# The last stage of an adaLN block with routed experts: two sums per batch added by transfers, by TensorE or by VectorE

## The chip, the core and the metric

The kernel runs on one core of a Trainium2 chip. The metric is the device time of one launch in microseconds (us). The kernel before took 437.91 us as the median of 3 runs (436.64 to 440.29). The profile comes from one further execution.

## The reference, cut to what matters

The block takes 8 batches of 256 tokens with 256 features, all in fp32. Attention adds to `x`; then comes a feed-forward part with 16 routed experts (each token goes to 4 of them) and one shared expert of width 352. Two of its lines are the subject of this document:

```
y = jnp.einsum('teh,ehd,te->td', h, w2, cw)          # the routed experts, weighted
z = jax.nn.silu(xf @ sw1) * (xf @ sw3) @ sw2         # the shared expert
...
x = x + gb * (y + z)                                 # gb: one row of 256 per batch
```

So each output needs the sum of a token's four expert results, the shared expert's result, one multiplication by the gate `gb`, and one addition of the residual `x`.

## The kernel before

**The work up to the last stage.** Attention and routing run first, on all engines, in an order that is written out by hand. Then tiles of 128 tokens of one expert each go through five steps: `fetch` (a load of sorted rows by the queue of SyncE, SP), `turn`, `up`, `flip` and `down` (TensorE with ScalarE and VectorE). `down` ends with a tile of 128 rows, and `add_some` (L1207) adds these to their tokens' rows in DRAM by an indirect transfer with addition, issued by GpSimd (POOL). To keep neighbouring additions apart there are two tables in DRAM, `sums[0]` and `sums[1]`, and the tiles go to them in turn. Each of the two holds a part of `y`, and both have to be added at the end. There are 70 such additions in the profiled execution. Transfers that POOL issues go through the queue q0 of the profile, those of SP through q1.

**The shared expert.** For batches 0 to 5 it is computed earlier and added to the residual `xs[b]` with its gate. For batches 6 and 7 (`NEXT` = 6) it is left to the end. `hidden(b0, 2, i)` (L1215) takes chunk `i` of three of the hidden width (128, 128 and 96 columns) for two batches at once: four matmuls with 512 columns (L1224), a Silu on ScalarE (L1230) and a product on VectorE (L1231) that makes the tile `hs`. `shared(b)` (L1235) takes the three `hs` tiles to one batch's result in PSUM, in six matmuls with 256 columns (L1240).

**The last stage (L1312 to L1337).** SP loads, for batch 0 to 7 in order, a quarter of a megabyte from `sums[0]` and another from `sums[1]` into the halves of a tile `got` (L1319), 16 loads in all. The loads wait for the last additions to DRAM. Meanwhile TensorE computes `hidden` and `shared` for batches 6 and 7. Then VectorE makes for each batch a pass `got[0] + got[1]` (L1330), for batches 6 and 7 another that adds the shared expert from PSUM (L1332), a pass that multiplies by the gate (L1333), and a pass that adds `xs[b]` (L1336). SP stores the result (L1337).

**What sets the order.** Up to the end of the first expert tiles the three compute engines follow the order of the code. In the last stage a scheduler of the compiler orders each engine's instructions by its own estimates, so VectorE mixes passes of several batches with those of `hidden`. Each engine then works through its queue in that order: an instruction that waits holds up all behind it. SP issues its 16 loads first and its 8 stores after them.

Of the kernel before, what the change touches and what calls it, by code (L numbers as in the profile page):

```python
# [9 lines left out]
F32 = mybir.dt.float32  # L10
# [4 lines left out]
ALU = mybir.AluOpType  # L15
# [3 lines left out]
P = 128  # L19
B, S, HID = 8, 256, 256  # L20
NT = S // P
# [31 lines left out]
SHC = [(c, min(P, SH - c)) for c in range(0, SH, P)]  # L53
# [8 lines left out]
NEXT = 6  # L62
# [12 lines left out]
BEHIND = mybir.DependencyInfo(mybir.DependencyClass.NoSync, mybir.DependencyReason.DATA)  # L75
# [3 lines left out]
def kernel(  # L79
# [18 lines left out]
    nc = tc.nc  # L98
# [18 lines left out]
    xs = []  # L117
# [3 lines left out]
    def load_x(b):  # L121
# [16 lines left out]
        out=bias_sb,  # L138
        in_=expert_bias.rearrange("(o e) -> o e", o=1).to_broadcast([P, E]),
# [7 lines left out]
    ident = const.tile([P, P], F32)  # L147
# [9 lines left out]
    for lo, n in ((0, P), (P, Q0)):  # L157
        nc.gpsimd.affine_select(
            out=maskb[:, lo : lo + n], in_=maskb[:, lo : lo + n], compare_op=ALU.is_ge, fill=HIDDEN,
# [3 lines left out]
            out=maskb[:, lo : lo + n], in_=maskb[:, lo : lo + n], compare_op=ALU.is_ge, fill=HIDDEN,  # L163
# [9 lines left out]
    for pr in probs:  # L173
# [7 lines left out]
        out=lowG, in_=lowG, compare_op=ALU.is_gt, fill=0.0,  # L181
# [6 lines left out]
        out=before, in_=before, compare_op=ALU.is_gt, fill=0.0,  # L188
# [11 lines left out]
    for m in range(SUMS):  # L200
# [4 lines left out]
            out=spread[:, m, :].rearrange("p (j d) -> p j d", d=D),  # L205
            in_=spread[:, m, :].rearrange("p (j d) -> p j d", d=D),
# [11 lines left out]
    def apart(ins, group):  # L218
# [12 lines left out]
    first = const.tile([P, E], F32)  # L231
    nc.gpsimd.iota(
        first, pattern=[[CAP, E]], base=1, channel_multiplier=0,
# [13 lines left out]
    start = const.tile([E, 1], F32)  # L247
    nc.gpsimd.iota(
        start, pattern=[[0, 1]], base=-E * CAP, channel_multiplier=CAP,
# [5 lines left out]
        out=upto, in_=upto, compare_op=ALU.is_ge, fill=0.0,  # L255
# [9 lines left out]
    sums = [tc.dram_tile([NTOK + P, HID], F32, name=f"sums_{i}") for i in range(2)]  # L265
# [76 lines left out]
    with ExitStack() as actx:  # L342
# [701 lines left out]
        for b in range(B):  # L1044
# [63 lines left out]
        ps_y = ctx.enter_context(tc.tile_pool(name="ps_y", bufs=2, space=PSUM))  # L1108
        small_ps[0] = ps_r
        gbs = gp.tile([P, B, HID], F32)  # L1110
        nc.sync.dma_start(
            out=gbs, in_=gates_d[1:2].rearrange("a b d -> a (b d)").to_broadcast([P, B * HID])
        )

        xts, hts, sels, zs = {}, {}, {}, {}
# [99 lines left out]
        def hidden(b0, nb, i):  # L1215

            c, n = SHC[i]
            pool, tag = ((ps_t, "t"), (ps_u, "u"), (ps_t, "t"))[i]
            pus = [
                pool.tile([P, 2, S], F32, tag=tag, name=f"us_{b0}_{i}_{a}")[:, 0:nb] for a in range(2)  # L1220
            ]
            for a in range(2):
                for k in range(NK):
                    nc.tensor.matmul(  # L1224
                        out=pus[a][:n], lhsT=sw13_sb[:, k, a, c : c + n],
                        rhs=h2T[:, k, b0 : b0 + nb, :],
                        start=(k == 0), stop=(k == NK - 1),
                    )
            h = fp.tile([P, 2, S], F32, tag="hs", name=f"hs_{b0}_{i}")[:, 0:nb]
            nc.scalar.activation(h[:n], pus[0][:n], AF.Silu)  # L1230
            nc.vector.tensor_tensor(h[:n], h[:n], pus[1][:n], ALU.mult)  # L1231
            for b in range(b0, b0 + nb):
                hids[b, i] = h[:, b - b0]

        def shared(b):  # L1235

            pz = ps_y.tile([P, NT, HID], F32, tag="y", name=f"pz_{b}")
            for t in range(NT):
                for i, (c, n) in enumerate(SHC):
                    nc.tensor.matmul(  # L1240
                        out=pz[:, t, :], lhsT=hids[b, i][:n, t * P : (t + 1) * P],
                        rhs=sw2_sb[:n, i, :],
                        start=(i == 0), stop=(i == len(SHC) - 1),
                    )
            return pz

# [8 lines left out]
        def shared_next(b):  # L1255

            pz = shared(b)
            nc.vector.tensor_tensor(
                pz, pz, gbs[:, b, :].unsqueeze(1).to_broadcast([P, NT, HID]), ALU.mult
            )  # L1260
            nc.vector.tensor_tensor(xs[b], xs[b], pz, ALU.add)
# [8 lines left out]
        def shared_some(b0):  # L1270

            for i in range(len(SHC)):
                hidden(b0, 2, i)
                yield
            for b in range(b0, b0 + 2):
                shared_next(b)
                yield
# [34 lines left out]
    tctx.close()  # L1312
    ep = ctx.enter_context(tc.tile_pool(name="ep", bufs=B))
    fp = ctx.enter_context(tc.tile_pool(name="fp_end", bufs=len(SHC)))
    gots = []
    for b in range(B):
        got = ep.tile([P, 2, NT, HID], F32, tag="got", name=f"got_{b}")
        for i in range(2):
            nc.sync.dma_start(  # L1319
                out=got[:, i], in_=sums[i][b * S : (b + 1) * S, :].rearrange("(p t) d -> p t d", p=P)  # L1320
            )
        gots.append(got)
    for b0 in range(NEXT, B, 2):
        for i in range(len(SHC)):
            hidden(b0, 2, i)
        for b in range(b0, b0 + 2):
            zs[b] = shared(b)
    for b, got in enumerate(gots):
        o = got[:, 0]
        nc.vector.tensor_tensor(o, got[:, 0], got[:, 1], ALU.add)  # L1330
        if b in zs:
            nc.vector.tensor_tensor(o, o, zs[b], ALU.add)  # L1332
        nc.vector.tensor_tensor(  # L1333
            o, o, gbs[:, b, :].unsqueeze(1).to_broadcast([P, NT, HID]), ALU.mult
        )
        nc.vector.tensor_tensor(o, o, xs[b], ALU.add)  # L1336
        nc.sync.dma_start(out=out[b].rearrange("(t p) d -> p t d", p=P), in_=o)  # L1337


# [54 lines left out]
```

## Time and profile before

| | |
|---|---|
| median of 3 runs (lowest, highest) | 437.91 us (436.64, 440.29) |
| the profiled execution's own time | 436.18 us |
| its span | 434.2 us |
| granted TensorE clock, mean over the span | 0.973 |
| busy share: PE, VectorE (DVE), GpSimd (POOL), ScalarE (ACT) | 91%, 59%, 55%, 44% |
| last POOL instruction ends | 404.05 us |
| first load of the last stage issued | 408.67 us |
| last VectorE pass ends | 430.88 us |

Times in views of the trace count from the start of the span, so the last stage is what lies between about 400 and 434 us. "PEclk" or "granted clock" is the share of full speed at which TensorE was let run. "PEld" is the load of weights into TensorE. A matmul in fp32 shows as two instructions, so 6 matmuls of `shared` are 12 rows. "Idle before" is what an engine waited before an instruction, and the arrow names what ended the wait. The share of DMA is the mean busy share of the core's 16 transfer engines; it can pass 1 a little where packets overlap.

### The profile page before, as it was taken

How to read it: one execution, taken by the hardware profiler on the slowest of the kernel's cores; microseconds unless marked ns; L12 is line 12 of the kernel's file. 1: busy time of each engine (PE TensorE's matmuls, PEld its weight loads, DVE VectorE, ACT ScalarE, POOL GpSimd, SP SyncE). 2: the span in 40 equal slices, each digit the busy share in tenths (PEclk: the TensorE clock that was granted, in tenths of full speed). 3: DMA queues.
4: the chain of work that ended last, by engine and by line, in shares of the span. 5: the costliest groups of instructions: out<-in, count | busy, mean ns of one | idle time of the engine just before them, and what ended most of it. 6: DMA issues, size and time to landing. Idle time of an engine off the chain costs nothing.

```text
span 434.2 us, 8867 instructions
## 1 busy us (share of the span) xinstructions
PE 396.6 (91%) x2790; PEld 282.3 (65%) x2790; DVE 256.5 (59%) x937; ACT 192.6 (44%) x445; POOL 239.3 (55%) x232
## 2 busy tenths in 40 slices
PE   3779999899999989799999999999999999997963
PEld 3445777677788855567776575667777777775332
DVE  4586887989887745456763343354445444443096
ACT  1446687777767743245432212134334344433100
POOL 8255444648878755056754346766666666656100
PEclk9998999999999999999999999999999999999778
DMA  8999996012131321535554226667766666675493
GB/s 257 368 362 306 323 231 171 2 54 61 63 103 61 110 95 61 175 109 130 141 129 110 54 53 103 77 109 122 115 107 116 117 104 120 113 116 79 95 381 128
DMA packets 53214, 60.05 MB, mean 138 GB/s; under 512 B 5304, under 2 KB 48176, under 8 KB 53040
## 3 DMA queue, kind: packets, MB, share of 16 engines
q1 hardware_dynamic: 40016, 40.86, 32.2%
q0 software_dynamic: 13152, 18.62, 23.5%
q8 instruction: 24, 0.39, 0.4%
q14 instruction: 22, 0.18, 0.1%
HBM read 31.77 MB, written 27.69 MB: 137 GB/s over the span
## 4 chain that ended last, share of the span: by engine, by line
PE 43%; DMA 8%; DVE 4%; issue 2%; ACT 1%; SPq 0%; DVEq 0%
PE u L1167 17%; PE py L1193 13%; DMA sums<-yr,to 5%; PE us L1224 4%; PE ph L1182 3%; PE xt L1135 3%; PE pz L1240 2%; DMA xr<-rows_d 2%; DMA got<-sums 1%; DVE got L1330 1%; DVE got L1333 1%; DVE got L1336 1%; DVE got L1332 0%; ACT L1174 0%; ACT L895 0%
## 5 line engine op out<-in xcount | busy, mean ns | idle before, releaser
L1207 POOL DMA_INDIRECT sums<-yr,to x70 | 109.6, 1565 | 54.3 <-DVE yr L1200 11.9
L1167 PE MATMUL u<-w,xT 128*128 x288 | 98.9, 467 | 2.2 <-ACT xT L1137 2.2
L976 POOL DMA_INDIRECT rows_d<-pay,idx x64 | 63.9, 998 | 64.6 <-PE ph L1182 24.2
L1193 PE MATMUL py<-w_sb,hT 88*128 x280 | 72.1, 380 | 0.0
L1167 PEld LDWEIGHTS u<-w,xT 128*128 128x128 f32 x288 | 49.9, 193 | 19.2 <-ACT xT L1137 2.4
L1137 ACT COPY xT<-xt 128x256 f32<-128x256 f32 x73 | 26.9, 372 | 60.7 <-PE xt L1135 60.7
L1175 DVE TENSOR_TENSOR h<-h,u 128x176 f32<-128x176 f32 x72 | 24.2, 337 | 47.3 <-ACT h L1174 47.1
L1193 PEld LDWEIGHTS py<-w_sb,hT 88*128 88x128 f32 x280 | 47.7, 190 | 3.8
L1174 ACT ACTIVATE h<-u 128x176 f32<-128x176 f32 x72 | 22.8, 317 | 57.9 <-PE u L1167 57.2
L1200 DVE TENSOR_SCALAR yr<-py,w 128x256 f32<-128x256 f32 x70 | 33.6, 479 | 11.1 <-PE py L1193 10.8
L1224 PE MATMUL us<-h2T,sw_sb 128*128 128x512 f32 (+1 forms) x72 | 35.6, 640 | 3.5 <-PEq L1306 2.7
L399 POOL TENSOR_TENSOR rstd<-rstd,nhalf 128x24 f32<-128x24 f32 x8 | 33.8, 4220 | 0.7
L1141 DVE SCALAR_TENSOR_TENSOR both<-eno,whose,xr 128x16 f32<-128x16 f32 x73 | 16.9, 232 | 27.2 <-DMA xr<-rows_d 26.9
L1182 PEld LDWEIGHTS ph<-ident,h 128*88 128x88 f32 x142 | 17.1, 122 | 21.4 <-issue 12.2
L516 PE MATMUL pq<-wqkv_sb,hT 128*128 128x384 f32 x64 | 27.7, 565 | 2.9 <-ACT hT L375 2.0
L1135 PE MATMUL xt<-ident,xr 128*128 128x128 f32 x146 | 28.2, 276 | 0.0
L1182 PE MATMUL ph<-ident,h 128*88 128x128 f32 x142 | 27.2, 274 | 0.6 <-DVE h L1175 0.6
L1224 PEld LDWEIGHTS us<-h2T,sw_sb 128*128 128x128 f32 (+1 forms) x72 | 13.8, 196 | 21.2 <-issue 19.2
L1184 ACT COPY hT<-ph 88x256 f32<-88x256 f32 x71 | 26.1, 367 | 2.5 <-PE ph L1182 2.2
L1135 PEld LDWEIGHTS xt<-ident,xr 128*128 128x128 f32 x146 | 20.4, 144 | 8.8 <-issue 2.9
L634 ACT ACTIVATE probs<-probs 128x640 f32<-128x640 f32 x32 | 23.6, 737 | 1.0
L631 ACT ACTIVATE probs<-sc 128x640 f32<-128x640 f32 x32 | 22.2, 694 | 4.1 <-PE sc L622 4.1
(231 smaller groups left out, 658.3 us busy)
## 6 DMA issues: line engine op xcount, KB each, us to landing
xr<-rows_d SPq DMA_DIRECT2D x75, 144.0 KB
w<-in_w_dram SPq DMA_DIRECT2D x16, 352.0 KB
sums<-none SPq DMA_DIRECT2D x2, 2176.0 KB
got<-sums SPq DMA_DIRECT2D x16, 256.0 KB
w_sb<-in_w_dram SPq DMA_DIRECT2D x8, 352.0 KB
rows_d<-none SPq DMA_DIRECT2D x1, 2304.0 KB
x<-in_x_dram SPq DMA_DIRECT2D x8, 256.0 KB
out_dram<-got SPq DMA_DIRECT2D x8, 256.0 KB
```

The lines of the kernel that those rows point to most:

```text
L399: in_turn("own", nc.gpsimd.tensor_tensor(out, out, nhalf[:, 0 : in_.shape[-1]], ALU.pow))
L516: ins = nc.tensor.matmul(out=pq[:, 0 : NH * D], lhsT=hT[:, k, t * P : (t + 1) * P], rhs=wqkv_sb[:, k, :], start=(k == 0), stop=(k == NK - 1),)
L976: ins = nc.gpsimd.indirect_dma_start(out=rows_d[:, :], out_offset=bass.IndirectOffsetOnAxis(ap=idx[:, t, k : k + 1], axis=0), in_=pay[:, t ...
L1135: nc.tensor.transpose(pt[:, k, :], x[:, k * P : (k + 1) * P], ident)
L1137: nc.scalar.copy(xT, pt)
L1167: ins = nc.tensor.matmul(out=pu, lhsT=xT[:, k, :], rhs=w13[:, k, bass.ds(e, 1), :].rearrange("p o h -> p (o h)"), start=(k == 0), stop=(k ...
L1182: nc.tensor.transpose(ph[:, i, :], h[:, i * HALF : (i + 1) * HALF], ident)
L1184: nc.scalar.copy(hT, ph)
L1193: nc.tensor.matmul(out=py, lhsT=h[:, i, :], rhs=w2_sb[:, i, bass.ds(e, 1), :].rearrange("p o d -> p (o d)"), start=(i == 0), stop=(i == 1),)
L1200: nc.vector.tensor_scalar(y, py, w, None, ALU.mult)
L1207: ins = nc.gpsimd.indirect_dma_start(out=sums[len(added) % 2][:, :], out_offset=bass.IndirectOffsetOnAxis(ap=to[:, 0:1], axis=0), in_=y, i ...
L1224: nc.tensor.matmul(out=pus[a][:n], lhsT=sw13_sb[:, k, a, c : c + n], rhs=h2T[:, k, b0 : b0 + nb, :], start=(k == 0), stop=(k == NK - 1),)
```

## The change

Only the last stage changes, and the functions `hidden` and `shared` for it.

- **Batches 2, 3, 4, 5.** SP loads only the first sum. The second one is added to it in SBUF by a transfer with addition that GpSimd issues (it waits until SP's load has landed). VectorE's pass L1330 is gone for these four.
- **Batches 6, 7.** Both sums are loaded as before. TensorE adds them into the PSUM tile of the shared expert: two matmuls of the identity with 512 columns each open the accumulation, and `shared` goes on in it. VectorE's passes L1330 and L1332 are gone for these two; the gate's multiplication reads PSUM.
- **Batches 0, 1.** As before, with three passes on VectorE.
- **Orders.** SP's loads come in the order 2, 3, 0, 4, 5, 1, 6, 7. VectorE's order is written out: products of `hidden` for chunks 0 and 1, batch 0, batch 1, product of chunk 2, batches 2, 3, 6, 4, 5, 7.

```diff
             h = fp.tile([P, 2, S], F32, tag="hs", name=f"hs_{b0}_{i}")[:, 0:nb]
             nc.scalar.activation(h[:n], pus[0][:n], AF.Silu)
-            nc.vector.tensor_tensor(h[:n], h[:n], pus[1][:n], ALU.mult)
...
+            return nc.vector.tensor_tensor(h[:n], h[:n], pus[1][:n], ALU.mult)
-        def shared(b):
+        def shared(b, pz=None):
+            first = pz is None
+            if first:
+                pz = ps_y.tile([P, NT, HID], F32, tag="y", name=f"pz_{b}")
...
-                        start=(i == 0), stop=(i == len(SHC) - 1),
+                        start=(first and i == 0), stop=(end if first else end and t == NT - 1),
...
+    order, order_v, by_dma = (2, 3, 0, 4, 5, 1, 6, 7), (0, 1, 2, 3, 6, 4, 5, 7), (2, 3, 4, 5)
+    for b in order:
+        got = gots[b] = ep.tile([P, 2, NT, HID], F32, tag="got", name=f"got_{b}")
+        nc.sync.dma_start(out=got[:, 0], in_=of(0, b))
+        if b in by_dma:
+            nc.gpsimd.dma_start(out=got[:, 0], in_=of(1, b), accum_op=ALU.add)
+        else:
+            nc.sync.dma_start(out=got[:, 1], in_=of(1, b))
...
+    def back(b):
+        got = gots[b]
+        y = o = got[:, 0]
+        if b in pos:
+            o = pos[b]
+        elif b not in by_dma:
+            behind(nc.vector.tensor_tensor(y, y, got[:, 1], ALU.add))
+        behind(nc.vector.tensor_tensor(
+            y, o, gbs[:, b, :].unsqueeze(1).to_broadcast([P, NT, HID]), ALU.mult
+        ))
+        behind(nc.vector.tensor_tensor(y, y, xs[b], ALU.add))
+        nc.sync.dma_start(out=out[b].rearrange("(t p) d -> p t d", p=P), in_=y)
+    pos = {}
+    for i in range(len(SHC)):
+        mult = hidden(NEXT, 2, i)
+        if i == len(SHC) - 1:
+            for b in order_v[:2]:
+                back(b)
+        behind(mult)
+    for b in range(NEXT, B):
+        o = pos[b] = ps_y.tile([P, NT, HID], F32, tag="y", name=f"po_{b}")
         for i in range(2):
+            nc.tensor.matmul(out=o, lhsT=ident, rhs=gots[b][:, i], start=(i == 0), stop=False)
+        shared(b, o)
+    for b in order_v[2:]:
+        back(b)
```

`of(i, b)` is batch `b`'s part of `sums[i]`. `behind` chains VectorE's instructions in the order in which it is called; it adds no semaphore.

More of the change, by code (lines that the diff above doesn't have):

```diff
@@ L1230, in hidden @@
             nc.scalar.activation(h[:n], pus[0][:n], AF.Silu)
-            nc.vector.tensor_tensor(h[:n], h[:n], pus[1][:n], ALU.mult)
             for b in range(b0, b0 + nb):
                 hids[b, i] = h[:, b - b0]
-        def shared(b):
-            pz = ps_y.tile([P, NT, HID], F32, tag="y", name=f"pz_{b}")
+            return nc.vector.tensor_tensor(h[:n], h[:n], pus[1][:n], ALU.mult)
[3 more added lines that the diff above has]
+                pz = ps_y.tile([P, NT, HID], F32, tag="y", name=f"pz_{b}")
             for t in range(NT):
                 for i, (c, n) in enumerate(SHC):
+                    end = i == len(SHC) - 1
                     nc.tensor.matmul(
@@ L1314 @@
     fp = ctx.enter_context(tc.tile_pool(name="fp_end", bufs=len(SHC)))
-    gots = []
-    for b in range(B):
-        got = ep.tile([P, 2, NT, HID], F32, tag="got", name=f"got_{b}")
-        for i in range(2):
[L1319 to L1337, printed above, removed]
+    gots = {}
+    order, order_v, by_dma = (2, 3, 0, 4, 5, 1, 6, 7), (0, 1, 2, 3, 6, 4, 5, 7), (2, 3, 4, 5)
@@ new lines, in of, with behind @@
+    def of(i, b):
+        return sums[i][b * S : (b + 1) * S, :].rearrange("(p t) d -> p t d", p=P)
+    for b in order:
[5 more added lines that the diff above has]
+            nc.sync.dma_start(out=got[:, 1], in_=of(1, b))
+    last_v = []
+    def behind(ins):
+        ins = getattr(ins, "ins", ins)
+        if last_v:
+            tc.add_manual_dep(ins, last_v[-1], BEHIND, reason="order of VectorE")
+        last_v.append(ins.name)
```

## The prediction, as it was put on record

> **What bounds the kernel now.** I read the chain that ended last first, cut to the end of the span (start, length, what):
>
> ```profile
> 385.72 22.74 DMA sums<-yr,to
> ...
> 408.67 0.33 SPq L1319
> ...
> 409.99 5.04 DMA got<-sums
> 415.03 0.02 issue
> 415.05 0.69 DVE got L1330
> ```
>
> The last additions to DRAM land at 408.46, the first load goes out at 408.67, and two batches' loads end the next wait at 415.03. From there the chain stays on VectorE. Its timeline says whether VectorE is idle anywhere:
>
> ```profile
> 412.40 0.69 DVE L1330 TENSOR_TENSOR got<-got 128x512 f32<-128x512 f32 x1 [12.89 <-DMA got<-sums]
> 413.01 0.68 DVE L1231 TENSOR_TENSOR hs<-hs,us 128x512 f32<-128x512 f32 x1
> 413.61 0.69 DVE L1333 TENSOR_TENSOR got<-got,gbs 128x512 f32<-128x512 f32 x1
> 415.05 0.69 DVE L1330 TENSOR_TENSOR got<-got 128x512 f32<-128x512 f32 x1 [0.76 <-DMA got<-sums]
> ...
> 420.47 0.68 DVE L1231 TENSOR_TENSOR hs<-hs,us 96x512 f32<-96x512 f32 x1
> ...
> 430.19 0.69 DVE L1336 TENSOR_TENSOR got<-got,x 128x512 f32<-128x512 f32 x1
> ```
>
> Starts are 0.60 us apart and no wait is shown after 415.05: 26 passes in 430.88 - 415.05 = 15.83 us, 0.605 a pass. So VectorE bounds the last stage now; after its last pass come 434.2 - 430.88 = 3.3 us of store. Then I asked how close the other two resources are, by windows (length; PE, PEld, DVE, ACT, POOL busy; granted clock, DMA share, GB/s), and by TensorE's timeline:
>
> ```profile
> 416.00:417.00 1.00, 0.00 (x0) 0.00 (x0) 1.00 (x3) 0.00 (x0) 0.00 (x0) 1.00 1.04 391
> 418.00:419.00 1.00, 0.80 (x2) 0.71 (x3) 1.00 (x3) 0.00 (x0) 0.00 (x0) 0.50 1.05 404
> 423.00:424.00 1.00, 1.00 (x4) 0.76 (x3) 1.00 (x2) 0.00 (x0) 0.00 (x0) 0.50 0.53 184
> 425.00:426.00 1.00, 1.00 (x6) 0.89 (x5) 1.00 (x3) 0.00 (x0) 0.00 (x0) 1.00 0.34 122
> ```
>
> ```profile
> 403.72 11.66 PE L1224 MATMUL us<-h2T,sw_sb 128*128 128x512 f32 x22 [0.30 <-PEq L1306]
> ...
> 421.20 5.91 PE L1240 MATMUL pz<-sw_sb,hs 96*128 96x256 f32 x18 [0.93 <-DVE hs L1231]
> ```
>
> The transfer engines are full from 410 to 423, and TensorE's clock is halved from 418 to 424.65. Its shared expert ends at 427.1 (421.20 + 5.91), under the cover of VectorE's other passes. Both have little room.
>
> **VectorE: passes removed.** Before, 29 passes: 8 x L1330, 2 x L1332, 8 x L1333, 8 x L1336, 3 products. Removed: four L1330 (batches 2 to 5), two L1330 and two L1332 (6, 7), so 8 x 0.605 = 4.8 us. But before, three passes ran ahead of 415.05; now only the two early products can (their Silus end at 409.24 and 410.86), since batch 0 is now third in SP's order: its loads are the 3rd and 4th, and the 4th landed at 415.03 before. So 19 passes remain from 415.05: 11.5 us, to 426.5. VectorE alone would end 4.3 us earlier. That holds only if nothing else is late.
>
> **Loads and added transfers.** At 391 to 408 GB/s a load of 262 KB costs 0.65 us of all 16 engines. SP's loads go from 16 to 12, so 2.6 us of engine time are removed. Four transfers with addition, of 262 KB each, come in. The trace has none into SBUF; the nearest row is the addition into DRAM. The last one runs alone:
>
> ```profile
> 404.50:405.00 0.50, 0.50 (x2) 0.29 (x1) 0.00 (x0) 0.00 (x0) 0.00 (x0) 0.50 0.96 53
> 405.00:405.50 0.50, 0.50 (x1) 0.04 (x1) 0.00 (x0) 0.00 (x0) 0.00 (x0) 0.50 0.94 145
> 405.50:406.00 0.50, 0.50 (x2) 0.34 (x1) 0.00 (x0) 0.00 (x0) 0.00 (x0) 0.50 0.43 64
> ```
>
> (0.96 + 0.94 + 0.43) x 0.5 = 1.17 us of all engines for 131 KB. Twice the bytes are at most 2.3 us. From below, two loads' worth of reading is 1.3. I take 1.75, the middle[...]. Four: 7.0 us (5.2 to 9.4), a net 4.4 more (2.6 to 6.8). POOL takes 1.56 us an addition in the trace (1.0 without addition, L976), and the bytes start 0.45 after it ends. So batch 2's addition, released near 411.8, starts moving at about 413.7; 3, 4 and 5 queue on POOL behind it, each behind its own load, and only VectorE's passes for these batches wait for them.
>
> Here a rule speaks against the change. The Trainium skill ("DMA: Bandwidth & Descriptors", Issuing engines are not separate DMA queues) says that transfers issued by GpSimd run on the same 16 engines and interleave with SP's. The trace agrees: from 387.75 to 389.5 a row load (147 KB) and one addition share the engines, and their time, 1.59 us, is about 0.36 (the load's bytes at full rate) plus 1.17. The load took 0.9 us where 0.36 was its due, so it had about 0.4 of the engines. With the share above 1 in such windows (1.07 to 1.28) I give SP's loads 0.6 of their old rate while additions are in flight (ends: 0.3 if the queues take turns packet by packet, 1.0 if the additions only fill gaps).
>
> By 413.7 some 1.2 MB, or 4.6 loads, have moved (326 GB/s from 410). At 0.6 each further load takes 1.08 us: the 8th is through at 417.4, the 9th at 418.5, the 12th at 421.7; 1.2 us later (0.85 to 1.8 by loads 2 and 4) it has landed. Batch 1 (7th, 8th): 418.6. Batch 6 (9th, 10th): 419.7 and 420.8. Without contention these are 417.8, 418.4 and 419.1, since SP's waits for slots ended at this pace before.
>
> **TensorE: work added.** A 512-column matmul takes 0.85 us at full clock (two rows 0.43 apart near 410), a 256-column one 0.43. Four identity matmuls add 3.4 to the shared expert's 12 x 0.43 = 5.1: 8.5 us at full clock, double when halved. And all of it moves behind batch 6's first load, because the identity opens the accumulation: before, the shared expert started at 415.21; now TensorE stands from 415.4 to 419.7. The clock will then be halved, as it was at 418 after a shorter stop. When does it come back? The skill ("TensorE: Matmul & The Clock Gate", Part 1) puts a busy window of about 3.4 us ahead of full clock, on a clock of its own. By the rule alone, 3.4 us cold do 1.7 us of work, 6.8 remain, end at 429.9. The row says 418.2 to 424.65 with gaps: TensorE's return inside a window costs more. I take the row, 424.65: 5 us cold, less some idling for load 10, do 2.3; 6.2 remain; end at 430.9. The third product no longer decides: it is queued behind batches 0 and 1 on VectorE, 418.6 + 3 x 0.605 + 0.6 = 421.0, in time for TensorE, which is in batch 6's identities until 422. If batch 1 were 2 us later, both batches' last matmuls would wait.
>
> **The sum.** TensorE ends with batch 7 at 430.9; two passes, 1.3 us with the last one's length: 432.2; store, 3.3: 435.5. The four additions end earlier: 7.0 us of engine time at half a share until 422 and alone after that end near 425, landed by 427 to 429, and their four passes are done by 430 in VectorE's order ahead of batch 7. So 435.5 against a span of 434.2: +1.3 us. The profiled execution ran 436.18 in all (2.0 around the span), a little below the median; +1.3 on the median is **439.2 us**. The 4.3 us that VectorE saves are eaten because the end passes to TensorE.
>
> **Rivals.** *The passes saved show in full.* For it: VectorE is gapless now. It needs batch 6's loads at 417.5, before the clock drops, so additions that take almost nothing from loads; then TensorE ends by 426 and VectorE at 426.5 to 427.2: -3.5 to -4.3 us, 433.6 to 434.4. Half of the effect, or a clock back at 421.3, gives 436. Against it: the full transfer engines. *The additions starve the loads (slower).* At a share of 0.3 and 1.75 us each, SP's loads move 1 for every 2.4 us from 413.7: batch 6's first lands near 424, TensorE starts cold, ends at 434.5 to 436, and the time is +5 to +7, 443 to 445. It decides from a share of about 0.4 down (load 9 at 422, TensorE ends at 433.6, +4.0). For it: 53 to 145 GB/s while an addition has the engines. Against: the row load above got more than 0.3. *The change doesn't do what it says:* if additions land after 431, their passes push batch 7's and the end is theirs; at 2.3 us each that starts to matter, 440 to 442. I count it with the slower one.
>
> **How the numbers follow.** Forecast case 0.55 (its own range 437 to 442), full or half saving 0.20 (433 to 437), starved 0.25 (441 to 447). One per cent, about what a measurement of this kernel can tell from no change, is 433.5 and 442.3. Faster: 0.4 of the second case, 0.08. Slower: 0.85 of the third and 0.08 of the first, 0.26. Within: 0.66. The range 434 to 445 leaves about one in ten on each side.
>
> **What would show it.** The identity matmuls start at 419 to 421 with a halved clock, waiting on loads; TensorE's last matmul ends at 430 to 432 and VectorE waits for it before batch 7; DMA share stays near 1 to 425 with GB/s under 350 between 414 and 422; POOL shows four transfers. Wrong if VectorE is gapless to 427, if the identities start before 418 at full clock, or if batches 4 and 5 wait for additions at the end.

## The result, and the profile after

The changed kernel takes **439.68 us** as the median of 20 runs (437.93 to 440.98), the kernel before on the same chip 436.88 us (435.29 to 440.29): a ratio of **1.0056, with a 95% interval of 1.0042 to 1.0070**. The medians differ by 2.8 us; the ratio makes it 2.4. The forecast was a small loss, 439.2 us or 1.3 us more. The loss came, and it is about twice as large.

The profiled execution of the changed kernel took 440.56 us, its span is 438.8 us at a mean granted clock of 0.975. Its chain of waits, cut to the end (start, length, what):

```profile
386.87 24.38 DMA sums<-yr,to
...
411.46 0.33 SPq L1328
...
415.16 7.41 DMA got<-sums
422.57 0.14 issue
422.71 3.97 PE po L1366 x4
426.68 2.91 PE po L1243 x12
429.59 1.72 PE po L1366 x4
431.31 2.61 PE po L1243 x12
433.92 0.02 issue
433.94 0.70 DVE got L1349
434.64 0.02 issue
434.67 0.69 DVE got L1352
```

L1328 and L1332 are now SP's loads, L1366 the identities, L1243 the shared expert's matmuls, L1348, L1349 and L1352 VectorE's sum, gate and residual. Before, the chain went from the loads straight to VectorE and stayed there. Now it goes from the loads to TensorE, runs through all that TensorE has left to do (the identities and the shared expert of both batches), and has only two VectorE passes at its end.

The first load goes out at 411.46, not at 408.67, because POOL's last addition into DRAM came out later in this execution; nothing up to there is changed. So I count from that load, "+" in what follows, and call **the stage** what lies between it and the end of the span: 434.2 - 408.67 = 25.5 us before, 438.8 - 411.46 = 27.3 after. One execution's stage is no median: on the chip of e0 below, a kernel's stage less that of the kernel before and the same difference of the medians disagree by up to 1.5 us.

VectorE's timeline shows what the saved passes became (start, length; the bracket is the idle time ahead and what ended it):

```profile
417.00 0.69 DVE L1348 TENSOR_TENSOR got<-got 128x512 f32<-128x512 f32 x1 [3.65 <-DMA got<-sums]
...
420.61 0.69 DVE L1348 TENSOR_TENSOR got<-got 128x512 f32<-128x512 f32 x1 [1.46 <-DMA got<-sums]
421.33 0.69 DVE L1349 TENSOR_TENSOR got<-got,gbs 128x512 f32<-128x512 f32 x1
422.06 0.69 DVE L1352 TENSOR_TENSOR got<-got,x 128x512 f32<-128x512 f32 x1
422.67 0.68 DVE L1233 TENSOR_TENSOR hs<-hs,us 96x512 f32<-96x512 f32 x1
...
424.83 0.69 DVE L1349 TENSOR_TENSOR got<-got,gbs 128x512 f32<-128x512 f32 x1 [0.16 <-DMA got<-sums]
...
429.62 0.69 DVE L1349 TENSOR_TENSOR got<-po,gbs 128x512 f32<-128x512 f32 x1 [3.37 <-PE po L1243]
...
433.94 0.69 DVE L1349 TENSOR_TENSOR got<-po,gbs 128x512 f32<-128x512 f32 x1 [0.24 <-PE po L1243]
```

VectorE makes 21 passes instead of 29, and now it stands: for loads at first, then 3.37 us for TensorE ahead of batch 6 and 0.24 us ahead of batch 7. TensorE's timeline has the other side, a stand of 7.79 us for a load, and then 3.97 us for batch 6's two identity matmuls (four rows):

```profile
422.71 3.97 PE L1366 MATMUL po<-got,ident 128*128 128x512 f32 x4 [7.79 <-DMA got<-sums]
```

The windows of the stretch (length; PE, PEld, DVE, ACT, POOL busy; granted clock, DMA share, GB/s) show both reasons why these are late and slow:

```profile
416.00:417.00 1.00, 0.00 (x0) 0.00 (x0) 0.00 (x1) 0.00 (x0) 0.65 (x1) 1.00 1.04 326
420.00:421.00 1.00, 0.00 (x0) 0.00 (x0) 0.39 (x1) 0.00 (x0) 0.13 (x1) 0.68 1.07 252
423.00:424.00 1.00, 1.00 (x2) 0.18 (x1) 0.96 (x3) 0.00 (x0) 0.00 (x0) 0.50 1.12 264
427.00:428.00 1.00, 1.00 (x6) 0.90 (x5) 0.00 (x0) 0.00 (x0) 0.00 (x0) 0.91 1.06 269
```

The transfer engines are full, yet move 252 to 269 GB/s where before they moved 391 to 404. That is the sum of both queues. The DMA view, cut to 420 to 427, has each alone (packets, MB, share of the engines' time):

```profile
q0 software_dynamic: 495, 0.92, 71.2%
q1 hardware_dynamic: 502, 0.90, 38.9%
```

In these 7 us SP's queue q1 moves 0.90 MB, 129 GB/s, a third of what it moved before. And the clock falls to 0.50 while TensorE stands, and comes back only some 4.5 us after it has restarted.

### The profile page after: what moved, and what is told of

It is laid out like the page before. It is cut to its first block, busy times and chain, and to the rows that moved or that the text cites. A ratio compares the mean times of both kernels' runs of the same rounds, so it can differ in the third digit from the quotient of the medians.

```text
span 438.8 us, 8875 instructions
## 1 busy us (share of the span) xinstructions
PE 398.6 (91%) x2798; PEld 283.1 (65%) x2798; DVE 252.2 (57%) x929; ACT 192.6 (44%) x445; POOL 243.2 (55%) x236
## 4 chain that ended last, share of the span: by engine, by line
PE 46%; DMA 9%; DVE 1%; SPq 1%; ACT 0%; issue 0%; DVEq 0%
PE u L1167 18%; PE py L1193 12%; DMA sums<-yr,to 6%; PE us L1224 4%; PE xt L1135 3%; PE ph L1182 3%; DMA xr<-rows_d 2%; PE pz L1243 2%; DMA got<-sums 2%; PE po L1366 1%; PE po L1243 1%; SPq L1328 1%; ACT L895 0%; SPq L1332 0%; DVE both L1141 0%
## 5 line engine op out<-in xcount | busy, mean ns | idle before, releaser
L976 POOL DMA_INDIRECT rows_d<-pay,idx x64 | 64.0, 1001 | 65.2 <-PE ph L1182 25.2
L1137 ACT COPY xT<-xt 128x256 f32<-128x256 f32 x73 | 26.9, 372 | 60.8 <-PE xt L1135 60.7
L1224 PE MATMUL us<-h2T,sw_sb 128*128 128x512 f32 (+1 forms) x72 | 34.1, 618 | 3.5 <-PEq L1309 2.7
L1184 ACT COPY hT<-ph 88x256 f32<-88x256 f32 x71 | 26.1, 367 | 3.2 <-PE ph L1182 2.8
L1135 PEld LDWEIGHTS xt<-ident,xr 128*128 128x128 f32 x146 | 20.5, 145 | 8.9 <-issue 2.9
L634 ACT ACTIVATE probs<-probs 128x640 f32<-128x640 f32 x32 | 23.6, 737 | 1.0
L631 ACT ACTIVATE probs<-sc 128x640 f32<-128x640 f32 x32 | 22.2, 694 | 3.7 <-PE sc L622 3.7
```

The costliest lines, as they stand in the source:

```text
L976: ins = nc.gpsimd.indirect_dma_start(out=rows_d[:, :], out_offset=bass.IndirectOffsetOnAxis(ap=idx[:, t, k : k + 1], axis=0), in_=pay[:, t ...
L1135: nc.tensor.transpose(pt[:, k, :], x[:, k * P : (k + 1) * P], ident)
L1137: nc.scalar.copy(xT, pt)
L1184: nc.scalar.copy(hT, ph)
L1224: nc.tensor.matmul(out=pus[a][:n], lhsT=sw13_sb[:, k, a, c : c + n], rhs=h2T[:, k, b0 : b0 + nb, :], start=(k == 0), stop=(k == NK - 1),)
```

## The experiments

Two theories. **The order theory:** the time is lost because the identities *open* the accumulation. All of TensorE's work then waits for batch 6's loads, meets a halved clock, and carries the end. **The transfer theory:** the time is lost to the added transfers, directly (batches 4 and 5 late at the end) or by starving SP's loads, that is, by slowing them. A third thing was open: whether the third product of `hidden`, queued behind batches 0 and 1, holds TensorE.

The runs used more than one chip. On one the kernel before took 436.58 us; there the unchanged copy of the changed kernel (e0), e4, e6 and e8 ran. e1, e2, e3 and e5 ran where it took 456.48, and e9 to e12 where it took 458.08. Each ratio is to the kernel before on the same chip. Landing times scatter between executions (batch 6's first load, with the transfers and in the same place of the order: +11.0 to +13.2), so "+" times are compared within one group.

**The changed kernel again (e0).**

> The changed kernel itself, beside the variants on the same chip, so that they have its stage and ratio there. From the record: ratio 1.0056 (1.0042 to 1.007), stage 27.3 us; the spread of load 9's landing (11.25 in its first trace, 12.4 in the one with fillers) says how far single stages wander.

Measured: 439.71 us, ratio 1.0075 (1.0045 to 1.0104). Stage 27.1; identities from +10.99, load 10 (batch 6's second) landed at +12.89, TensorE ended at +22.16. The first profile is typical.

**The transfers and orders alone (e1).** The transfers and the orders of the change stay. TensorE computes the shared expert as before; VectorE makes L1330 and L1332's passes for batches 6 and 7 again.

```diff
+        if b not in by_dma:
+            behind(nc.vector.tensor_tensor(y, y, got[:, 1], ALU.add))
         if b in pos:
-            o = pos[b]
-        elif b not in by_dma:
-            behind(nc.vector.tensor_tensor(y, y, got[:, 1], ALU.add))
+            behind(nc.vector.tensor_tensor(y, y, pos[b], ALU.add))
...
     for b in range(NEXT, B):
-        o = pos[b] = ps_y.tile([P, NT, HID], F32, tag="y", name=f"po_{b}")
-        for i in range(2):
-            nc.tensor.matmul(out=o, lhsT=ident, rhs=gots[b][:, i], start=(i == 0), stop=False)
-        shared(b, o)
+        pos[b] = shared(b)
```

> One part alone: the four added transfers and the orders stay, but batches 6 and 7 get their three extra passes on VectorE back and TensorE's identities go. Stage = time from the first load to the end of the span: 25.5 us in the kernel before, 27.3 in the changed one. Theory (the end passed to TensorE, which opens late and cold with 3.4 us more work): TensorE is off the end, VectorE has 20 passes left when batch 1 is there (9.15 us after the first load); in dependent pairs they start 0.73 apart in the changed kernel's trace, in mixed order 0.60, so 20 x 0.605 + 12 x 0.12 = 13.5 us, then 3.4 of store: stage 26.1, 1.2 less than the changed kernel, about 1.001 to 1.002 of the kernel before. Rival (the added transfers hold the end by themselves): stage stays at 27 or more and VectorE waits for batches 4 and 5.

Measured: 459.98 against 456.48 us, ratio 1.0073 (1.0040 to 1.0105); stage 27.8 (26.1 expected). Without TensorE's sums the kernel loses as much as with the whole change. How is in TensorE's timeline and VectorE's:

```profile
442.42 5.72 PE L1243 MATMUL pz<-sw_sb,hs 96*128 96x256 f32 x16 [8.54 <-DVE hs L1233]
```

```profile
446.24 0.69 DVE L1348 TENSOR_TENSOR got<-got,pz 128x512 f32<-128x512 f32 x1 [0.61 <-PE pz L1243]
```

Batch 1 landed at +10.06. The third product stands behind its passes, at +12.1, and TensorE waits 8.54 us for that product and restarts cold. But it holds VectorE up by 0.61 us only. The rest is VectorE: 20 passes from batch 1's landing to +24.30 are 14.2 us, and no pass waits for batch 4's or 5's transfer. So the direct form of the transfer theory falls: the transfers don't hold the end, the *late batch 1* does, and VectorE has nearly as much left behind it (14.2 us) as before behind batch 1 (15.8). Before, batch 1 was there at +6.4. Most of its lateness is SP's order, in which its loads are the seventh and eighth: without the transfers (e2, next) it lands at +8.93.

**Without the transfers (e2).** The four additions are left out, so the outputs of batches 2 to 5 lack their second sum; all else is the changed kernel.

```diff
-        if b in by_dma:
-            nc.gpsimd.dma_start(out=got[:, 0], in_=of(1, b), accum_op=ALU.add)
-        else:
+        if b not in by_dma:
             nc.sync.dma_start(out=got[:, 1], in_=of(1, b))
```

> The changed kernel without the four added transfers (batches 2 to 5 leave the second sum out, which takes their work away and no other). Theory: SP's loads come at their old pace, batch 6's first load lands 9.7 us after the first load's issue instead of 11.25, its second at 10.4 instead of 13.1; TensorE then ends 1.5 to 2.5 us earlier and with it the stage: 25 to 25.8 instead of 27.3. Rival (transfers cost the loads nothing, TensorE's own work and clock do it all): stage 27. Rival (transfers are the whole cause): stage 23 to 24, VectorE without a wait to the end.

Measured: 457.33 us, ratio 1.0033 (1.0004 to 1.0062); stage 26.3. TensorE's timeline and one window:

```profile
438.45 3.75 PE L1364 MATMUL po<-got,ident 128*128 128x512 f32 x4 [3.87 <-DMA got<-sums]
```

```profile
437.85:438.85 1.00, 0.40 (x1) 0.43 (x2) 0.97 (x2) 0.00 (x0) 0.00 (x0) 0.50 1.05 395
```

The loads are back at 395 GB/s, and batch 6's first load lands at +9.6; in e5, in the same group and with the transfers, at +12.4. So the transfers do starve the loads, and that costs some 0.4% (1.0073 and 1.0071 in e1 and e5, 1.0033 here; the intervals overlap, so the rates and landing times are the firmer witness). But even with transfers that cost *nothing* the kernel is not faster than before: TensorE still stands for 3.87 us, the clock is still 0.50, and the end is still TensorE's at +21.3. The stage was expected at 25 to 25.8; it measured 26.3, since the expectation let the clock come back sooner.

**Batches 6 and 7 loaded early, transfers kept (e3).**

```diff
-    order, order_v, by_dma = (2, 3, 0, 4, 5, 1, 6, 7), (0, 1, 2, 3, 6, 4, 5, 7), (2, 3, 4, 5)
+    order, order_v, by_dma = (0, 6, 2, 3, 7, 4, 5, 1), (0, 6, 1, 7, 2, 3, 4, 5), (2, 3, 4, 5)
...
-        if i == len(SHC) - 1:
-            for b in order_v[:2]:
-                back(b)
         behind(mult)
...
-    for b in order_v[2:]:
+    for b in order_v:
         back(b)
```

> The changed kernel with batch 6 second and batch 7 fifth in SP's order, batch 1 last, and VectorE's order changed to match (third product first, then batches 0, 6, 1, 7, 2, 3, 4, 5). TensorE opens about 6 us after the first load instead of 11.25, at full or nearly full clock, and is done by 15 to 16. Theory (the late opening is what costs): the end goes back to VectorE and the added transfers, stage 25 to 25.5, about 2 us less than the changed kernel. Rival (the added transfers bound the stage by themselves, here their loads come later): stage 27 or more, with VectorE waiting for batches 2 to 5.

Measured: 456.67 us, ratio 0.9982 (0.9951 to 1.0013); stage 25.2, as expected. TensorE's timeline:

```profile
433.93 1.96 PE L1363 MATMUL po<-got,ident 128*128 128x512 f32 x4 [2.43 <-DMA got<-sums]
```

The same four rows start at +6.1 and take 1.96 us instead of 3.97; TensorE is done at +14.9. All four transfers and all identities are still there, and the loss is gone. So neither makes a loss by its mere presence: the place in the order does. This run doesn't tell the two theories apart further, because batch 6's loads now also run ahead of the transfers; e6 below does. There is no gain either: VectorE now waits 4.2 us for TensorE ahead of batch 6, which comes second in its order.

**TensorE's part alone, in a good order (e4).** No transfers with addition; loads in the order 0, 6, 1, 7, 2, 3, 4, 5, VectorE's batches 0, 1, 6, 2, 3, 7, 4, 5, the products first as in e3.

> The other part alone: no added transfers (16 loads by SP), TensorE adds the sums of batches 6 and 7, whose loads are moved up to second and fourth place, third product first on VectorE. Theory: with its loads early TensorE is done by 15 us after the first load and off the end; VectorE has 22 passes left from 3.7 to 4.3 us on, 13.3 us, plus about 1.7 for dependent pairs and 2.5 of gaps before batches 1 and 6: ends at 21, stage 24.3 to 24.8, about 0.998 of the kernel before. Rival (TensorE's sum costs more than it saves wherever its loads lie): stage above 25.5.

Measured: 436.23 against 436.58 us, ratio 0.9987 (0.9971 to 1.0003); stage 24.2. Identities from +5.3 at full clock, TensorE done at +14.2, VectorE at +20.9 with waits of 0.53 and 0.46 us. VectorE has four passes less than before and nearly no waits, and yet gains at most 1.4 us of stage. Its timeline shows why:

```profile
415.41 0.69 DVE L1349 TENSOR_TENSOR got<-got,gbs 128x512 f32<-128x512 f32 x1
416.13 0.69 DVE L1352 TENSOR_TENSOR got<-got,x 128x512 f32<-128x512 f32 x1
```

Starts are 0.72 us apart where the second pass reads the first one's result, 0.60 where it does not. The scheduler of the kernel before mixed the batches and paid 0.605 for each; the written-out order takes batch by batch and pays 0.69 on average.

**Keeping TensorE warm, two tries (e5, e9).** Matmuls on data that is there already fill TensorE's stand; their result is not used.

```diff
+    fill = ps_r.tile([P, 512], F32, tag="mm", name="fill")[:, 0:S]
+    for i in range(15):
+        nc.tensor.matmul(out=fill, lhsT=ident, rhs=hids[NEXT, 1], start=True, stop=True)
     for b in range(NEXT, B):
```

(e9: 20 of them.)

> The changed kernel with 15 matmuls of 256 columns put between the hidden part and the identities, their result unused; they keep TensorE busy for about 6.4 of the 7.8 us in which it stood. If the halved clock is part of the cause, the identities and batch 6's matmuls run at full clock, limited by load 10 at 13.1 us: TensorE ends 1.3 to 1.6 us earlier, stage 25.8 to 26.0. If the loads alone set TensorE's end, the stage stays at 27.3; if the fillers overrun, it is longer.

Measured: 459.21 us, ratio 1.0071 (1.0038 to 1.0104), stage 28.9. Inconclusive: the fillers ended at +9.1, the loads landed at +12.4 and +14.3, and the second half of batch 6's identities was cold again.

> The fillers again, 20 matmuls of 256 columns, so that TensorE is busy until about 12 us after the first load[...]; their result is unused. Theory (the halved clock costs 1.3 to 1.6 us of TensorE's 11.2): behind load 10 at about 13 us only 7.8 us at full clock remain instead of 9.3, TensorE ends near 20.9 instead of 22.2, stage 25.8 to 26.2, ratio about 1.004 to 1.005. If the clock costs nothing here, stage 27.1 and ratio 1.0075; if the fillers overrun the loads, more.

Measured: 462.28 us, ratio 1.0064 (1.0024 to 1.0104), stage 27.5. Now the clock stays at 1.00:

```profile
447.86 1.12 PE L1369 MATMUL po<-got,ident 128*128 128x512 f32 x2 [0.90 <-DMA got<-sums]
...
451.42 1.88 PE L1369 MATMUL po<-got,ident 128*128 128x512 f32 x4
```

From load 10 (+14.55) to TensorE's end (+22.58) it takes 8.03 us. The stage misses the 25.8 to 26.2 expected because load 10 landed at +14.55 and not at about +13.

**Only the third product moved ahead (e10).** The edit of e3 without its first two lines: orders as in the change.

> The changed kernel with the third product ahead of batch 0 on VectorE, the one other edit that the kernel with the shared expert first has. By the prediction the product does not decide (it is done at 11.7 us, TensorE asks for it at 15): stage 26.9 to 27.3, ratio as the changed kernel's, 1.006 to 1.008. If it did decide, stage 26 or less.

Measured: 463.42 us, ratio 1.0107 (1.0063 to 1.0151); stage 29.7, where 26.9 to 27.3 was expected: both of batch 6's loads landed some 1.7 us later than in the first profile. TensorE's timeline:

```profile
446.52 4.02 PE L1363 MATMUL po<-got,ident 128*128 128x512 f32 x4 [9.12 <-DMA got<-sums]
```

The product is done at +4.5 and the identities start at +12.9 all the same, cold: the product decided nothing. Beside e9, on the same chip, this gives the price of the clock: from load 10 to TensorE's end 24.68 - 14.81 = 9.87 us here, 8.03 there, so 1.84 us. Here the clock came back 5.7 us after the restart. In the changed kernel, where that took 4.5 us, the same stretch is 433.92 - 424.6 = 9.3 us, so about 1.3 us is the price there.

**The shared expert opens, the identities close (e6).** The same work, transfers and orders; the third product goes first.

```diff
-        if i == len(SHC) - 1:
-            for b in order_v[:2]:
-                back(b)
         behind(mult)
     for b in range(NEXT, B):
-        o = pos[b] = ps_y.tile([P, NT, HID], F32, tag="y", name=f"po_{b}")
+        pos[b] = shared(b, None, True)
+    for b in range(NEXT, B):
         for i in range(2):
-            nc.tensor.matmul(out=o, lhsT=ident, rhs=gots[b][:, i], start=(i == 0), stop=False)
-        shared(b, o)
-    for b in order_v[2:]:
+            nc.tensor.matmul(out=pos[b], lhsT=ident, rhs=gots[b][:, i], start=False, stop=(i == 1))
+    for b in order_v:
         back(b)
```

(`shared` starts each tile once and leaves its last matmul open.)

> The changed kernel with TensorE's accumulation turned round: the shared expert of batches 6 and 7 first, right behind the hidden part, the four identities last; for that the third product goes ahead of batch 0 on VectorE. Loads, added transfers and amount of work unchanged. Theory (it is the opening by the identity that puts all of TensorE's work behind load 9): 5.1 us of shared expert are done by 9 us after the first load, only 1.7 to 3.4 us of identities stay behind the loads, batch 6 is ready at 15, batch 7 at 18; VectorE ends at 20 to 21, stage 23.6 to 24.5, about 3 us less than the changed kernel and 1 to 2 less than the kernel before. Rival (added transfers bound the stage): stage 26 or more, with VectorE waiting for batches 4 and 5.

Measured: 436.66 against 436.58 us, ratio 1.0001 (0.9982 to 1.0020). The profile's stage, 26.3, misses the 23.6 to 24.5 expected. That execution took 438.09 us, 1.4 above the median, and in it batch 6's first load landed at +13.2 instead of +11.0 and batch 1 at +11.5 instead of +8.9. What is left of TensorE's work then is short, cold, and paced by loads that land 2.0 us apart:

```profile
423.36 7.12 PE L1364 MATMUL pz<-got,ident 128*128 128x512 f32 x8 [3.96 <-DMA got<-sums]
```

```profile
427.50 0.69 DVE L1349 TENSOR_TENSOR got<-pz,gbs 128x512 f32<-128x512 f32 x1 [1.01 <-PE pz L1364]
```

Even so, VectorE waits for TensorE 1.01 us, where e0's waits are 3.55 and 0.24. By the medians this edit gives back 439.71 - 436.66 = 3.1 us, all that the change lost on that chip. Since transfers, loads and amount of work are those of the change, and the third product decided nothing (e10), it is the order of the accumulation that made the loss. Why the loads came 2 us later in the profiled execution is not explained.

**More sums by TensorE, no transfers, mixed passes (e8, e11).** What the experiments point to: no transfers with addition (they starve the loads), the shared expert opens, TensorE sums the four batches that are loaded last (two of them in further PSUM tiles), and VectorE's passes are mixed as the scheduler did.

```diff
+    order, order_v, by_dma = (0, 1, 2, 3, 6, 4, 7, 5), (), ()
...
+    pos, by_pe = {}, order[4:]
...
+    add(order[0])
+    gated_(order[0])
+    add(order[1])
+    for k in range(B):
+        finish(order[k])
+        if k + 1 < B:
+            gated_(order[k + 1])
+        if k + 2 < B:
+            add(order[k + 2])
```

(`add`, `gated_` and `finish` are the passes L1348, L1349 and L1352; `add` is empty for TensorE's batches. e11: TensorE's batches are 6, 7, 5, and the loads come in the order 0, 1, 2, 3, 6, 7, 4, 5.)

> A version built from the theory: no added transfers; SP's 16 loads in the order 0, 1, 2, 3, 6, 4, 7, 5; TensorE adds both sums of four batches (6, 4, 7, 5), behind the shared expert; VectorE's 23 passes mixed so that no pass follows the one it depends on. The last load lands 14.3 us after the first one's issue as in the kernel before, one identity and two passes follow: VectorE ends at 17 to 18, stage 20.7 to 21.5, 4 to 5 us less than the kernel before, ratio 0.990. Rival (identities cost TensorE more at half the clock than VectorE's passes): stage 23 or more, VectorE waiting for TensorE.

Measured: **433.37 against 436.58 us, ratio 0.9933 (0.9911 to 0.9956)**: faster than both kernels. Stage 22.0 (20.7 to 21.5 expected). Its chain:

```profile
413.27 6.18 DMA got<-sums
419.46 0.04 issue
419.50 1.98 PE pz L1352 x4
421.48 1.72 PE po L1352 x4
423.20 1.72 PE pz L1352 x4
424.92 1.73 PE po L1352 x4
426.65 0.02 issue
426.67 0.70 DVE got L1361
```

TensorE stands 1.1 us only, its clock stays at full, 1.72 us a batch, and it sets the end, as in the change; VectorE waits 0.30 us ahead of each of the last three batches. What each of the edits put together here is worth by itself was not measured.

> The version with four batches by TensorE, now three (6, 7, 5; loads 0, 1, 2, 3, 6, 7, 4, 5). In the other one VectorE waited 0.3 us for TensorE before each of the last three batches, identities 1.72 us a batch. Here VectorE has one pass more and TensorE 1.7 us less: VectorE ends at 18.2 to 18.5 instead of 18.8, stage 21.4 to 21.7, ratio 0.992 to 0.993. If loads bound the end, the same as with four.

Measured: 456.85 against 458.08 us, ratio 0.9961 (0.9922 to 1.0000), where 0.992 to 0.993 was expected; stage 21.7, as expected. The intervals overlap and the chips differ: three or four batches is not told apart.

**e4 with mixed passes (e12).**

> The kernel with TensorE's sums alone (loads 0, 6, 1, 7, ...), with VectorE's passes of neighbouring batches mixed, no pass right behind the one it depends on except at three places. 14 of its passes started 0.72 after the one they depend on, mixed ones 0.60: 11 x 0.12 = 1.3 us less, stage 22.8 to 23.2 instead of 24.15, ratio 0.995 to 0.996 instead of 0.9987. Rival (the gaps of loads swallow it): no change.

Measured: 456.38 us, ratio 0.9983 (0.9953 to 1.0013). The stage, 25.0, misses. The mean spacing fell as expected, from 0.69 to 0.625 us (13.1 us for 21 passes without waits); but in this execution the third product came at +7.3, with all passes queued behind it, against +4.0 in e4. TensorE had begun `hidden` only 5.4 us ahead of the first load, in e4 8.8 us ahead. This execution was also the slowest of its 12, 459.34 us. As a gain in time the mix is not shown.

## Why the prediction held

The mechanism was right: VectorE's saved passes are eaten because the end passes to TensorE. That the steps agree so well is in part luck. By the prediction's own steps:

| step, from the first load | predicted | measured |
|---|---|---|
| the transfers' bytes begin to move | 413.7 - 408.67 = 5.0 | 8.5 |
| rate of SP's queue beside them, share of the old rate | 0.6 | 0.33 |
| batch 6's first load, identities start | 419.7 - 408.67 = 11.0 | 11.25 |
| its second load landed | 12.1 | 13.1 |
| TensorE ends | 22.2 | 22.5 |
| last VectorE pass ends | 23.5 | 23.9 |
| store | 3.3 | 3.4 |
| stage | 26.8 | 27.3 |

**Loads and transfers: two errors that cancelled.** The queue of POOL's transfers, q0, in the DMA view cut to 411 to 439:

```profile
q1 hardware_dynamic: 3904, 5.24, 56.7%
q0 software_dynamic: 576, 1.05, 20.5%
```

20.5% of 28 us is 5.7 us for four, **1.43 us each**: below the 1.75 taken, inside its bounds, near the reading of two loads (1.3). The other two terms were mis-sized. Once the transfers were under way, SP's queue kept 129 GB/s of some 391, 0.33 of its old rate, and both queues moved almost the same number of packets (502 and 495). That is the end of 0.3 that the prediction had set aside, in which the queues take turns packet by packet. Its witness for more, the row load at 387.75, says little: 0.07 of its 0.15 MB had moved before the addition's first packets, after 388.5. But q0 had moved only 14 of its 576 packets by 420, that is by +8.5. POOL issued the first transfer at 414.80, and the bytes came some 4 us after that instruction's end, not 0.45. By then SP's queue had moved 2.24 MB, 8.5 loads' worth, where the prediction gave it 4.6. A late start at full pace and a smaller share afterwards brought load 9 to the forecast time; load 10 came 1.9 us behind it instead of 1.1. Why the transfers start so late is open. The line's own view shows that they are long in landing:

```profile
L1330 POOL DMA_DIRECT2D got<-sums x4: 867/934/1072, 414.8 to 419.1; - x4
...
DMA to landing us min/median/max: 8.4/8.7/9.1
```

This hurts nobody, as predicted: batch 3 waited 0.16 us, batches 4 and 5 not at all.

**The clock.** The prediction let a row of the kernel before stand against the Trainium skill ("TensorE: Matmul & The Clock Gate", Part 1), which puts a busy window of about 3.4 us ahead of full clock. Measured: restart at 422.71, full clock at about 427.2, so 4.5 us; 5 were taken. The traces do show such a window. Read in steps of 0.1 us, the clock of the changed kernel changes at -8.2, -4.8, +8.9 and +15.7, which are 3.4, 13.7 and 6.8 us apart, whole multiples of 3.4; it is so in every kept trace. The full clock came back at the end of the first such stretch in which TensorE worked throughout. So the cold time depends on where in a stretch the restart falls: 4.4 us in e0, 5.7 in e10, 5.8 in e2, 6.3 in e6. The 5 us were a fair middle; that they came within 0.5 is luck too. The cold stretch costs about 1.3 us here, 1.84 in e10.

**TensorE's work.** 11.2 us from the first identity to the end, predicted and measured; but the parts differ: load 10 landed 1.0 us later, the cold stretch was 0.5 us shorter.

**VectorE: another mis-sized term.** 0.605 us a pass was carried over from a mixed order to one where each pass reads the last one's result: 0.72 to 0.73. With TensorE the bound this was hidden in the change. In e1 and e4, where VectorE carries the end, it is what ate much of the gain, so "VectorE alone would end 4.3 us earlier" was too much: 19 passes at 0.69 are 13.1 us, not 11.5, which leaves 2.7. Nor could the 19 passes start at once: 16 of the changed kernel's passes start with batch 1's first, and batch 1 came at +9.15, not at +6.4 as before.

**The rivals.** *The passes saved show in full* needed batch 6 loaded before the clock drops; e3 made that so, and the ratio was 0.9982, since VectorE then waits elsewhere and has dependent passes. *The additions starve the loads* was right about the share: 0.33 lies below the 0.4 from which it was to decide. It didn't decide, because the starving began 3.5 us later than it supposed. *Additions land after 431* did not happen.

**What stays open.** The medians differ by 2.8 us here (2.4 by the ratio) and by 3.1 with e0, the stages by 1.8 and 1.6: what makes up the rest was not found; it is within what single executions vary. Why landing times of the same loads differ by 2 us between executions (e6 against e0) is not settled.

## What to carry to other kernels

Let a PSUM accumulation open with what is ready first and add the late arrivals last: the same matmuls in the other order were worth 3 us here, since less of TensorE's work waits for the late loads. Before a sum is moved to another engine or queue, ask what the new place waits for and what shares its resource; a transfer with addition takes its time from the loads that the other engines wait for. When two forecast terms are guesses, such as a start and a share here, check each against the trace, for a right sum can hide two wrong terms. When an order is written out by hand, keep two batches' passes mixed as the scheduler did.

## What the runs showed that was not expected

- A VectorE pass of 128x512 fp32 starts 0.60 us after an independent one and 0.72 to 0.73 after one whose result it reads. With e12's mix the mean fell to 0.625.
- A transfer of 256 KB with addition into SBUF costs the 16 transfer engines 1.43 us, more than twice a load's 0.65, and lands 8.4 to 9.1 us after its issue beside loads; while such transfers run, full engines move 250 to 270 GB/s instead of about 395, half of it by either queue (0.92 and 0.90 MB in 7 us).
- The length of a stand alone did not say whether TensorE keeps its clock. It restarted at full clock after stands of 1.1 us (e8), 2.4 (e3) and 3.3 (e5, halved 1.9 us later), at half after 2.4 (the kernel before), 3.9 (e2) and more. What fits is how much of one 3.4 us stretch was stood: the clock fell at the end of a stretch with 2.2 us of stand (before, the one to +9.3) and 2.3 (e5, to +14.3), and held after one with 1.8 (e5, to +10.9).
